# Routing of a mixture of experts: a moved square root, a comparison in another element order, added products and an early Gelu

## The chip, the cores and the metric

The kernel runs on one core of one Trainium2 chip. The metric is the device time of one execution in microseconds; lower is better. The engines of a core are TensorE (PE for its products, PEld for its weight loads), VectorE (DVE), ScalarE (ACT), GpSimd (POOL) and SyncE (SP, which here only issues DMAs). Each runs its own queue in order; semaphores tie them together.

## The reference

The input is x[2, 256, 64, 64]. Two layers follow: area attention with a gated recurrence, and convolutions with a state-space scan, then the mixture of experts that this change is about. Cut to that last part:

```python
# t: 8192 tokens of 256 values, E = 8 experts, hidden size 512
xf = (t - mean(t)) / sqrt(var(t) + 1e-5)           # per token
probs = softmax(xf @ gate_w + gate_b)              # [8192, 8]
top2_vals, top2_idx = top_k(probs, 2)
for e in range(8):
    h = gelu(xf @ W1[e] + b1[e])                   # exact Gelu
    out += weight_of_e[:, None] * (h @ W2[e] + b2[e])
t = t + out
```

## The kernel before

The experts are computed only for the tokens that chose them. Every token has two picks; the picks are laid out in blocks of 256 rows (`RB`), all rows of a block for one expert, at most 71 blocks (`NBLK`, rounded up to `NB` = 72), of which 68 are computed here. The part has four stages, all within `experts`.

**Normalise and choose** (`normalise`, `choose`). The tokens lie as 64 tiles of 128 (`TILES`), in 16 groups of four (`K`). Per group, `turn` transposes on PE and ACT copies the result to `x_turned`; `measure` takes the sums of the variance on DVE; `gates` multiplies four groups at a time by the gate's weights; `turn_gates` transposes these products back and DVE copies them to `logits`. For each half of the tiles, `root_in` computes the variance on DVE and its square root on ACT (L1818), and `root_out` the reciprocal. `scale` then normalises each group, three tiles of four on ACT (L1835) and one on POOL (L1831), and SP writes it to a table of rows in memory (`rows`, L1838). The order of all this is written out by hand (the engine queues follow the program). `choose` picks the two experts of each token on DVE.

**Slots.** Two products (L1972, operands `both` with `every` and `behind`) count how many tokens chose each expert before each token; from that DVE computes the slot of every pick: a block number `hi` and a place in the block `lo`. POOL then fetches the weights of the first three blocks (`wt`).

**The table loop** (L2030 to L2049). It inverts the slots: for each block and place, which token sits there. Sixteen rounds, each for four tiles. In a round DVE compares `hi` with the numbers 0 to 71 (`high`, L2033), ACT scales the result by the partition's number (L2038) and eight times by the tile's number (L2041) into `named`, DVE compares `lo` with the numbers 0 to 255 eight times (`low`, L2043), and PE multiplies `low` by `named` into `table` (L2045), 16 products. `high` and `named` have two buffers, `low` eight. These tiles take over the memory of the normalised tokens `xt`, so the first comparison waits until the last copy of tokens is written out.

```python
high = p4.tile([P, K, 2, NB], BF16, name="high")
nc.vector.tensor_tensor(
    high, place[:, :NB].unsqueeze(1).unsqueeze(1).to_broadcast([P, K, 2, NB]),
    hi[:, t0 : t0 + K].unsqueeze(3).to_broadcast([P, K, 2, NB]), ALU.is_equal,
)
```

Behind it `exponents` computes the softmax's exponentials on ACT (L1928 to L1930), and DVE turns the table into the indices `xi` and `ri`.

**Blocks and combination** (`run_blocks`, `combine`). For each block POOL gathers its tokens (`xg`), PE transposes them (`px`, L2085), DVE copies (L2087), PE multiplies by the first weights (`ph`, L2097) in four parts, ACT applies Gelu to each part (L2099), and PE multiplies by the second weights (`py`, L2107). The products of a block are interleaved with those of the block before it; the first block has none before it. A part's first product waits for the Gelu of the part before. At the end `combine` weighs the two results of each token and adds them to the input.

Of the kernel before, what the change touches and what calls it, by code (L numbers as in the profile page):

```python
# [10 lines left out]
F32 = mybir.dt.float32  # L11
BF16 = mybir.dt.bfloat16
I32 = mybir.dt.int32
AF = mybir.ActivationFunctionType
ALU = mybir.AluOpType
# [3 lines left out]
P = 128  # L19
# [13 lines left out]
E, HID = 8, 512  # L33

TB, RB = 512, 256


_WIDTHS = [
# [1648 lines left out]
def experts(tc, sh, ap, out, half, left):  # L1687
# [12 lines left out]
    nc, tok = tc.nc, sh.tok  # L1700
    NH, T, K = HID // P, B * N, TB // P
    NBLK = 2 * T // RB + E - 1
    TILES, J = T // P, RB // P

    OFTEN = 2 * T // RB + E // 2
    NB = NBLK + NBLK % 2
    with ExitStack() as ctx:
        cp = ctx.enter_context(tc.tile_pool(name="e_const", bufs=1))
# [16 lines left out]
        def iota(name, shape, pattern, base=0, step=0):  # L1725
            t = cp.tile(shape, F32, name=name)
            nc.gpsimd.iota(t, pattern, base=base, channel_multiplier=step, allow_small_or_imprecise_dtypes=True)
            return t
# [3 lines left out]
        numbers = iota("numbers", [P, RB], [[1, RB]])  # L1732
        place = cp.tile([P, RB], BF16, name="place")
        nc.vector.tensor_copy(place, numbers)
        me = iota("me", [P, 1], [[0, 1]], step=1)
        me1 = iota("me1", [P, 1], [[0, 1]], base=1, step=1)
# [3 lines left out]
        every = cp.tile([P, P], BF16, name="every")  # L1740
# [14 lines left out]
        wi = cp.tile([P, NBLK], I32, name="wi")  # L1755
        used = cp.tile([1, 1], I32, name="used")

        ex = cp.tile([P, TILES, E], F32, name="ex")
        best, total = (cp.tile([P, TILES], F32, name=n) for n in ("best", "total"))
        work = cp.tile([P, 2, TILES], F32, name="work")  # L1760
        held = ctx.enter_context(ExitStack())
# [10 lines left out]
        def normalise(p2, logits, halves):  # L1772


            with ExitStack() as own:
# [15 lines left out]
                def group(g):  # L1791
                    return slice(g * K, g * K + K)

                def turn(g):
                    turned = ps.tile([P, 2, K, P], F32, name="turned")
                    for c in range(2):
                        for k in range(K):
                            nc.tensor.transpose(turned[:, c, k], tok[:, g * K + k, c * P : c * P + P], sh.ident)
                    nc.scalar.copy(x[:, :, group(g)], turned)

                def measure(g):
                    for t in range(g * K, g * K + K):
                        for c in (0, 1) if t in left else (1,):
                            nc.vector.bn_stats(half[:, t, c], tok[:, t, c * P : c * P + P])

                def root_in(i):


                    at = slice(i * TILES // 2, (i + 1) * TILES // 2)
                    records = half[:, at].rearrange("p t c (i k) -> p t (c i) k", k=3)  # L1810
                    means, m, a = records[:, :, :, 1], mean[:, at], away[:, at]
                    nc.vector.tensor_reduce(m, means, AX.X, ALU.add)
                    nc.vector.tensor_scalar(m, m, 0.25, None, ALU.mult)
                    nc.vector.tensor_tensor(a, means, m.unsqueeze(2).to_broadcast([P, TILES // 2, 4]), ALU.subtract)
                    nc.vector.tensor_tensor(a, a, a, ALU.mult)
                    nc.vector.scalar_tensor_tensor(a, a, 64.0, records[:, :, :, 2], ALU.mult, ALU.add)
                    nc.vector.tensor_reduce(var[:, at], a, AX.X, ALU.add)
                    nc.scalar.activation(inv[:, at], var[:, at], AF.Sqrt, scale=1.0 / C, bias=sh.eps5)  # L1818

                def root_out(i):  # L1820
# [19 lines left out]
                def gates(q):  # L1840

                    pe = pg.tile([P, TB], F32, name="by_expert", bufs=2)
                    for c in range(2):
                        for j in range(4):
                            nc.tensor.matmul(
                                pe[32 * j : 32 * j + 32], gate[:, c], x[:, c, group(4 * q + j)],
                                start=c == 0, stop=c == 1, tile_position=(0, 32 * j),
                            )
                    return q, pe

                def take_gates(q, pe):
                    mine = pn.tile([P, TB], F32, name="by_expert_s", bufs=1)
                    nc.vector.tensor_copy(mine, pe)
                    return q, mine

                def turn_gates(q, mine):
                    pt = pg.tile([P, K, P], F32, name="by_token")
                    for k in range(K):
                        nc.tensor.transpose(pt[:, k], mine[:, k * P : k * P + P], sh.ident)
                    nc.vector.tensor_copy(  # L1860
                        logits[:, 16 * q : 16 * q + 16].rearrange("p (j k) e -> p j k e", k=K),
                        pt.rearrange("p k (j e) -> p j k e", e=32)[:, :, :, :E],
                    )
# [5 lines left out]
                for g in range(TILES // K):  # L1869
                    turn(g)  # L1870
                    if g == 4:
                        for i in range(8):
                            measure(i)
                        centre_gate()
                    if g == 5:
                        ready = take_gates(*gates(0))
                        root_in(0)
                        for i in range(8, 10):
                            measure(i)
                    if g == 6:  # L1880
                        turn_gates(*ready)
                    if g == 7:
                        root_out(0)
                        for i in range(10, 13):
                            measure(i)
                    if g == 9:
                        ready = take_gates(*gates(1))
                        for i in range(13, 16):
                            measure(i)
                    if g == 10:  # L1890
                        turn_gates(*ready)
                        halves[0]()
                    if g == 13:
                        ready = take_gates(*gates(2))
                        root_in(1)
                last = gates(3)
                turn_gates(*ready)
                ready = take_gates(*last)
                root_out(1)
# [26 lines left out]
        def exponents(pr):  # L1926

            nc.scalar.activation(one, going[:, 0, 0:1], AF.Exp)  # L1928
            nc.scalar.activation(ex, pr, AF.Exp)
            nc.scalar.activation(best, best, AF.Exp)  # L1930

        def weigh():
            nc.vector.tensor_reduce(total, ex, AX.X, ALU.add)
# [17 lines left out]
        def route():  # L1951
            with ExitStack() as own:
# [9 lines left out]
                p4 = own.enter_context(tc.tile_pool(name="e_r4", bufs=2))  # L1962
# [6 lines left out]
                rest = ps.tile([P, E * TILES], F32, name="rest")  # L1969
                turned = both.rearrange("p t e -> p e t")  # L1970
# [8 lines left out]
                n = p1.tile([P, E], F32, name="n")  # L1979
# [13 lines left out]
                at = left.rearrange("p t e -> p (t e)").rearrange("p (e t) -> p e t", e=E)  # L1993
                nc.vector.tensor_tensor(at.rearrange("p e t -> p (e t)"), scanned, rest, ALU.add)
                nc.vector.tensor_tensor(at, at, off.unsqueeze(2).to_broadcast([P, E, TILES]), ALU.add)
                at = at.rearrange("p e t -> p t e")
# [6 lines left out]
                hi = p1.tile([P, TILES, 2], BF16, name="hi")  # L2003
# [25 lines left out]

                table = ps.tile([P, J, 512], F32, name="table")  # L2030
                for t0 in range(0, TILES, K):
                    high = p4.tile([P, K, 2, NB], BF16, name="high")
                    nc.vector.tensor_tensor(  # L2033
                        high, place[:, :NB].unsqueeze(1).unsqueeze(1).to_broadcast([P, K, 2, NB]),
                        hi[:, t0 : t0 + K].unsqueeze(3).to_broadcast([P, K, 2, NB]), ALU.is_equal,
                    )
                    named = p4.tile([P, K, 2, 2, NB], BF16, name="named")
                    nc.scalar.mul(named[:, :, :, 1], high, me1)  # L2038
                    for t in range(t0, t0 + K):
                        for i in range(2):  # L2040
                            nc.scalar.mul(named[:, t - t0, i, 0], high[:, t - t0, i], float(t + TILES * i))  # L2041
                            low = p4.tile([P, RB], BF16, name="low", bufs=8)
                            nc.vector.tensor_scalar(low, place, lo[:, t, i : i + 1], None, ALU.is_equal)  # L2043
                            for j in range(J):
                                nc.tensor.matmul(  # L2045
                                    table[:, j, : 2 * NB], low[:, j * P : j * P + P],
                                    named[:, t - t0, i].rearrange("p k n -> p (k n)"),
                                    start=t == 0 and i == 0, stop=t == TILES - 1 and i == 1,
                                )  # L2049
                exponents(pr)  # L2050
                tile_of, inner = (table[:, :, k * NB : k * NB + NBLK] for k in range(2))
                tokens = p1.tile([P, J, NBLK], F32, name="tokens")
# [298 lines left out]
```

## Time and profile before

| | |
|---|---|
| median of 3 runs | 2871.01 us (2867.4 to 2874.39) |
| the profiled execution | 2871.29 us, span 2869.4 us |
| mean granted TensorE clock | 0.958 |
| busy: PE, DVE, ACT, POOL | 91%, 68%, 54%, 44% of the span |
| normalise and choose, slots | 2158.0 to 2218.45 us |
| table loop | 2218.45 to 2255.2 us |
| indices, first gathers, first blocks | 2255.2 to 2281.9 us |
| remaining blocks | 2281.9 to 2790 us |
| combination | 2790 to 2869.4 us |

Times in the profile are microseconds from the span's start. A row of a group or of the timeline gives when it starts, how long it was busy, the engine and the line, and in brackets how long its engine sat idle before it and what ended that. The granted clock is the share of full speed that TensorE was given. PE's busy share says little by itself, since products are pipelined.

### The profile page before, as it was taken

Reading aid. Unit: us, or ns where it says so; the run is one execution under the profiler, and the core shown is the slowest. Engines: PE = TensorE matmul, PEld = TensorE weight load, DVE = VectorE, ACT = ScalarE, POOL = GpSimd, SP = SyncE. Lnnn points to the kernel's source line nnn. Section 1 sums busy time; section 2 is a strip of 40 time slices with the busy share of each in tenths; the row PEclk is TensorE's granted clock in tenths of the full one; section 3 lists DMA queues with packets and bytes.
Section 4 is the critical chain, followed back from the end, with each engine's and each line's share of the span. In section 5 each row is a group of like instructions: output and inputs, shape, how many; then the busy total and the mean of one; then the engine's idle time right before and its main releaser. Section 6 shows DMA issues by size and latency. Waiting matters only on the chain.

```text
span 2869.4 us, 45738 instructions
## 1 busy us (share of the span) xinstructions
PE 2621.8 (91%) x17062; PEld 1502.7 (52%) x17062; DVE 1939.3 (68%) x3768; ACT 1542.8 (54%) x2623; POOL 1250.7 (44%) x1164
## 2 busy tenths in 40 slices
PE   7899999999999999997899999868895799999984
PEld 2233333333333333322899999724443588888873
DVE  4788888888888888886666667698887512221116
ACT  2567676776777676763444555576636522222223
POOL 1445445453544545452230000187761166666651
PEclk9999999999999999999899999999997799999995
DMA  3576767767767667777230000045543266666648
GB/s 133 102 138 124 139 129 133 139 130 133 137 132 135 131 130 140 133 140 144 84 155 1 1 2 1 12 124 137 143 129 138 85 222 232 220 234 220 233 171 342
DMA packets 104826, 388.15 MB, mean 135 GB/s; under 512 B 19656, under 2 KB 20560, under 8 KB 94864
## 3 DMA queue, kind: packets, MB, share of 16 engines
q0 software_dynamic: 71488, 293.00, 43.3%
q1 hardware_dynamic: 31872, 87.86, 9.5%
q10 hardware_dynamic: 1232, 4.25, 0.4%
q8 instruction: 137, 2.24, 0.3%
q14 instruction: 97, 0.79, 0.1%
HBM read 173.30 MB, written 43.58 MB: 76 GB/s over the span
## 4 chain that ended last, share of the span: by engine, by line
PE 77%; DVE 10%; issue 4%; DMA 3%; ACT 3%; POOL 2%; SPq 0%; ACTq 0%; DVEq 0%; POOLq 0%
PE ps L301 10%; PE ph L2097 9%; PE av_o L415 8%; PE py L2107 8%; PE po L169 8%; PE z L824 7%; PE ps L402 7%; PE z L836 7%; PE ps L397 3%; DVE hs L1569 2%; PE yp L1579 2%; DMA sx<-ex 2%; PE po L181 1%; PE px L2085 1%; PE po L415 1%
## 5 line engine op out<-in xcount | busy, mean ns | idle before, releaser
L371 DVE SCALAR_TENSOR_TENSOR acc<-vh,w_pe,acc 128x1008 f32<-128x1008 f32 (+7 forms) x384 | 483.3, 1262 | 8.3
L619 POOL DMA_DIRECT2D sx<-ex x320 | 276.8, 951 | 458.5 <-ACT ex L409 162.6
L409 ACT ACTIVATE ex<-ps 128x1024 f32<-128x1024 f32 x384 | 373.9, 1026 | 138.0 <-issue 56.1
L317 DVE CUSTOM_DVE_ANT_0 more<-ps,more 128x512 f32<-128x512 f32 x480 | 303.0, 687 | 132.5 <-PE ps L301 124.6
L2099 ACT ACTIVATE act<-ph,wt 128x256 f32<-128x256 f32 x272 | 128.9, 474 | 388.4 <-PE ph L2097 385.2
L2087 DVE COPY xt<-px 128x512 f32<-128x512 f32 x68 | 47.0, 692 | 397.7 <-PE px L2085 397.7
L2097 PE MATMUL ph<-xt,wt 128*128 128x256 f32 x1088 | 293.0, 392 | 4.9 <-ACT act L2099 3.0
L402 PE MATMUL ps<-q,k 32*128 32x512 f32 x2048 | 286.4, 602 | 0.0
L2107 PE MATMUL py<-wt,act 128*128 128x256 f32 x1088 | 279.6, 380 | 0.0
L614 POOL TENSOR_TENSOR sx<-sx,ex 128x1024 f32<-128x1024 f32 x64 | 152.3, 2380 | 220.7 <-PE ps L301 172.7
L313 ACT ACTIVATE more<-ps 128x1024 f32<-128x1024 f32 x240 | 233.5, 1029 | 18.1 <-ACT sx L409 5.9
L2097 PEld LDWEIGHTS ph<-xt,wt 128*128 128x128 f32 x1088 | 191.5, 192 | 68.0 <-DVE xt L2087 23.9
L824 PE MATMUL z<-xs,u 128*128 128x128 f32 x1872 | 223.2, 276 | 0.0
L415 PE MATMUL av_o<-ex,vt 128*32 128x512 f32 x1536 | 212.3, 609 | 6.1 <-ACT ex L409 5.9
L824 PEld LDWEIGHTS z<-xs,u 128*128 128x128 f32 x1872 | 216.9, 193 | 0.2 <-issue 0.2
L2107 PEld LDWEIGHTS py<-wt,act 128*128 128x128 f32 x1088 | 202.2, 191 | 24.9
L848 ACT ACTIVATE t<-z,bias 128x128 f32<-128x128 f32 x468 | 136.3, 361 | 145.8 <-PE z L836 145.7
L2122 POOL DMA_INDIRECT results<-y,ri x136 | 138.0, 1015 | 140.7 <-DVE y L2115 118.9
L301 PE MATMUL ps<-k,q 32*128 32x512 f32 x1088 | 195.6, 639 | 2.1 <-DVE nm L307 1.3
L836 PE MATMUL z<-xs,v 128*128 128x128 f32 x1512 | 179.6, 275 | 0.0
L836 PEld LDWEIGHTS z<-xs,v 128*128 128x128 f32 x1512 | 174.1, 192 | 0.2 <-DVE xs L855 0.2
L1576 POOL TENSOR_TENSOR cs<-hs,cs 128x1024 f32<-128x1024 f32 x63 | 148.6, 2361 | 55.1 <-DVE hs L1569 32.6
(432 smaller groups left out, 4530.5 us busy)
## 6 DMA issues: line engine op xcount, KB each, us to landing
sx<-ex POOLq DMA_DIRECT2D x320, 512.0 KB
cs<-c_rows SPq DMA_DIRECT2D x128, 256.0 KB
y<-results SPq DMA_DIRECT2D x32, 512.0 KB
x<-xrows SPq DMA_DIRECT2D x8, 1024.0 KB
rows<-xt SPq DMA_DIRECT2D x16, 512.0 KB
out_x<-res POOLq DMA_DIRECT2D x15, 512.0 KB
xrows<-xn SPq DMA_DIRECT2D x24, 256.0 KB
x<-in_x SPq DMA_DIRECT2D x4, 1024.0 KB
```

The costliest lines, as they stand in the source:

```text
L301: made.append(nc.tensor.matmul(tiles[h // 2][:, h % 2], qs[G, i // HM][head(h), i % HM * P : (i % HM + 1) * P], keys[head(h)], start=True, ...
L313: nc.scalar.activation(held["more"][j], tiles[j], AF.Relu)
L317: nc.vector.tensor_tensor_reduce(more, tiles[h // 2][:, h % 2], more, -1.0, 3.0e38, ALU.add, ALU.min, accum_out=nms[G][:, 0, h, i : i + 1],)
L371: mark(nc.vector.scalar_tensor_tensor(part, vh[:, c, 2 + r0 + dy : 2 + r1 + dy, w0 + dx : w1 + dx], w_pe[:, c, k : k + 1], part, ALU.mult, ...
L402: nc.tensor.matmul(tiles[h // 2][:, h % 2], k[head(h), m % HM * P : (m % HM + 1) * P], qs[G, n][head(h)], start=False, stop=True, tile_pos ...
L409: nc.scalar.activation(exs[i], tiles[i], AF.Exp, scale=HD**-0.5)
L415: nc.tensor.matmul(to[head(h)], lhs, exs[h // 2][:, h % 2], start=first, stop=last, tile_position=(0, HD * h))
L619: nc.gpsimd.dma_start(total[i], exs[i], accum_op=ALU.add)
L824: nc.tensor.matmul(z[c][:, g, :m], u[:, k, c, g], xt[:, k], start=g == GATES[0] and k == 0, stop=False, skip_group_check=True,)
L836: nc.tensor.matmul(z[c][:, g, :m], v[:, k, c, g], h[:, k], start=False, stop=k == 1, skip_group_check=True,)
L2097: nc.tensor.matmul(ph[:, hc], wt[:, at : at + P], xt[:, c], start=c == 0, stop=c == 1)
L2107: nc.tensor.matmul(py[:, j], act[:, hc, j * P : j * P + P], wt[:, at : at + C], start=hc == 0, stop=hc == NH - 1,)
```

## The change

Four things, all before the blocks:

- The square root of each half leaves `root_in` and becomes a function of its own, `root`. For the first half it is called right behind `root_in(0)`, as before. For the second it is called behind the last `gates`, so that on ACT it stands behind the copies of the last two groups.
- The comparison `high` is laid out with the 72 numbers outermost and the eight picks innermost. Its first operand is no longer a broadcast but a stored array `counted`, written once by POOL; it shares the memory of `ex`, which is used later. `high` being in another order, ACT reads it with a step of eight elements at both of its lines.
- Behind the table loop PE makes 28 products of `every` and `turned` (a view of `both`) into `rest`, whose value is not used any more.
- Behind the exponentials ACT computes a Gelu of a constant into a cell of `total`, which is overwritten later. The load of Gelu's table stands before it.

```diff
+WARM_UP = 28
...
-        ex = cp.tile([P, TILES, E], F32, name="ex")
+        held_by_both = cp.tile([P, 2 * TILES * E], BF16, name="ex")
+        ex = held_by_both.bitcast(F32).rearrange("p (t e) -> p t e", e=E)
+        counted = held_by_both[:, : NB * K * 2].rearrange("p (n k i) -> p n k i", k=K, i=2)
+        nc.gpsimd.tensor_copy(counted, numbers[:, :NB].unsqueeze(2).unsqueeze(2).to_broadcast([P, NB, K, 2]))
...
                     nc.vector.tensor_reduce(var[:, at], a, AX.X, ALU.add)
+
+                def root(i):
+
+                    at = slice(i * TILES // 2, (i + 1) * TILES // 2)
                     nc.scalar.activation(inv[:, at], var[:, at], AF.Sqrt, scale=1.0 / C, bias=sh.eps5)
...
                         root_in(0)
+                        root(0)
...
                         root_in(1)
                 last = gates(3)
+                root(1)
                 turn_gates(*ready)
...
             nc.scalar.activation(best, best, AF.Exp)
+            nc.scalar.activation(total[:, 0:1], sh.eps5, AF.Gelu)
...
-                    high = p4.tile([P, K, 2, NB], BF16, name="high")
+                    high = p4.tile([P, NB, K, 2], BF16, name="high")
                     nc.vector.tensor_tensor(
-                        high, place[:, :NB].unsqueeze(1).unsqueeze(1).to_broadcast([P, K, 2, NB]),
-                        hi[:, t0 : t0 + K].unsqueeze(3).to_broadcast([P, K, 2, NB]), ALU.is_equal,
+                        high, counted,
+                        hi[:, t0 : t0 + K].unsqueeze(1).to_broadcast([P, NB, K, 2]), ALU.is_equal,
                     )
                     named = p4.tile([P, K, 2, 2, NB], BF16, name="named")
-                    nc.scalar.mul(named[:, :, :, 1], high, me1)
+                    nc.scalar.mul(named[:, :, :, 1], high.rearrange("p n k i -> p k i n"), me1)
...
-                            nc.scalar.mul(named[:, t - t0, i, 0], high[:, t - t0, i], float(t + TILES * i))
+                            nc.scalar.mul(named[:, t - t0, i, 0], high[:, :, t - t0, i], float(t + TILES * i))
...
+                for _ in range(WARM_UP):
+                    nc.tensor.matmul(rest, every, turned, start=True, stop=True)
                 exponents(pr)
```

## The prediction

> **What bounds the kernel now.** I read the page's 40 slices first: TensorE is 90% busy everywhere except between slices 29 and 32 and at the end, and all edits lie in the first of these stretches (2158 to 2282 us), the experts' routing. A table of windows over it:
>
> ```profile
> 2158.00:2218.45 60.45, 32.90 (x214) 20.17 (x214) 46.33 (x162) 39.74 (x66) 11.30 (x20) 0.76 0.36 139
> 2218.45:2255.20 36.75, 24.59 (x256) 22.83 (x256) 35.93 (x144) 32.18 (x145) 2.39 (x3) 0.84 0.26 98
> 2255.20:2281.90 26.70, 15.64 (x38) 10.42 (x38) 3.15 (x8) 5.52 (x10) 8.52 (x9) 0.55 0.25 84
> 2281.90:2790.00 508.10, 506.10 (x2412) 415.66 (x2411) 110.61 (x170) 126.48 (x267) 321.97 (x334) 1.00 0.62 218
> ```
>
> Columns: stretch, length, busy PE, PEld, DVE, ACT, POOL, granted clock, DMA share, GB/s. The first row is normalising and choosing, the second the table loop, where DVE never rests (35.93 of 36.75), the third the first blocks at a clock of 0.55, the fourth the blocks, PE without a gap. Whatever the first three gain or lose arrives whole at the end. The chain of waits says what joins them:
>
> ```profile
> 2215.41 2.63 DMA rows<-xt
> ...
> 2218.45 0.76 DVE high L2033
> ...
> 2259.30 2.73 DMA xg<-rows,xi
> ...
> 2265.97 1.28 ACT L2099
> ```
>
> The loop starts when the last token copy has been written (its tiles take over that memory), not when DVE's own chain ends (2217.50); the blocks start when the gathers land; the first Gelu waits for a table load.
>
> **The square root.** The timeline before the loop:
>
> ```profile
> 2189.62 0.32 ACT L1818 ACTIVATE inv<-var,eps 128x32 f32<-128x32 f32 x1 [8.40 <-DVE var L1817]
> 2189.85 1.90 ACT L1799 COPY x_turned<-turned 128x1024 f32<-128x1024 f32 x2
> ...
> 2191.65 23.70 ACT L1835 ACTIVATE xt<-x,less,inv 128x256 f32<-128x256 f32 x48
> ```
>
> ACT waits 8.40 us at the second root (the first is not moved past anything) and holds two copies behind it; PE's last gate products wait 5.99 us for those. Moved behind them, the root still starts at 2189.62, when DVE has the variance, but the token copies follow at 2190.0: 1.65 us earlier. DVE gains more: it met the third turned gates at 2196.36 and would meet them at 2189.6, so the indices come about 6.7 us earlier, at 2210.7. That lets POOL issue the three weight gathers (3.5 MB) at about 2212 in place of 2217.74, and their data moved 1.8 us after the issue: at 2213.8, some 0.75 MB of token rows are still to be written at the 415 GB/s that the windows show as the most. Shared evenly the rows finish 1.3 us late. Bounds: -1.7 (no collision) to +1.5 (rows get a third); I take -0.4 us.
>
> **The comparison.** One of 16 rounds:
>
> ```profile
> 2236.41 0.74 DVE L2033 TENSOR_TENSOR high<-place,hi 128x576 bf16<-128x576 bf16 x1
> 2237.08 1.64 DVE L2043 TENSOR_SCALAR low<-place,lo 128x256 bf16<-128x256 bf16 x8
> 2237.25 0.78 ACT L2038 ACTIVATE named<-high,me 128x576 bf16<-128x576 bf16 x1 [0.24 <-PE table L2045]
> 2237.93 1.31 ACT L2041 ACTIVATE named<-high 128x72 bf16<-128x72 bf16 x8
> 2238.22 1.35 PE L2045 MATMUL table<-named,low 128*128 128x144 bf16 x16 [0.62 <-ACT named L2041]
> ```
>
> The round is 2.24 us, DVE's: 0.67 from `high` to the first `low`, then eight at 0.196. ACT needs 0.68 and eight at 0.1525, 1.90 us. At two elements a tick `high` loses 288 elements of 1.01 ns (744 ns for 576 against 304 for 142 at L2055): 0.29 us, a round of 1.95 on DVE, -4.6 us over 16 rounds, if ACT keeps 1.90. It may not. `high` now lies with its 72 numbers outermost, so ACT reads all 1152 elements of a round at a step of 8 bf16, 16 bytes. ACT has no such read in the trace; others have. The operand `both` of L1972 is read at just that step:
>
> ```profile
> L1972 PE MATMUL count<-both,every x1: 1057/1057/1057, 2205.1 to 2205.1; 128*128 128x512 bf16 x1
> ...
> L1558 PE MATMUL bn<-s_b,spread x128: 377/381/634, 1881.3 to 2145.4; 96*128 96x512 bf16 x128
> ```
>
> Minimum, median, maximum in ns. At half clock (0.50 in its window) the product with steps takes 1057 ns; a contiguous one of 512 columns takes 634 at most, its value at half clock: +0.83 ns an element. DVE's read in steps of 64 words at L1999 takes 1041 ns where L1995, contiguous and as long, takes 730: +0.61. PE's stationary loads at L743, also 64 words, come 146 ns apart at full clock against 109 contiguous: +0.29. ACT's round is then 2.24, 2.61 or 2.86 us; below, 1.90. Two of three say ACT takes the bound, and I take 0.70 ns, between them: 2.71 us, +0.47 in 16 rounds, **+7.5 us** (ends -4.6 and +9.9). PE (1.35 to 2.1 us a round) and DVE (1.95) hide under it. POOL's new copy of 576 numbers, about 1.3 us by its 555 ns for 256 elements, falls into POOL's idle 14.45 us before 2172.86: nothing; without that cover it would be those 1.3 us. Its result shares memory with `ex`, so the exponentials also wait for the last comparison, which is over 2 us before them.
>
> The Trainium skill (SBUF — State Buffer, in the section on door 1, the port swizzle) speaks against this edit and for it at once. It says lines are 16 bytes and an access to a new line each time pays, yet calls a step of eight bf16 free. L1972 decides that for PE: not free. Read the second way, the loop would bring -4.6 us and the sum would be 2865.6.
>
> **The products and Gelu's table.** 28 products of 512 columns go behind the table in PE's queue; the first block's transposes queue behind them. Let T be the loop's end. Before, PE waited 5.69 us and the second gather landed at T+6.84, so that much is free. How long are 28? Contiguous they came 0.22 us apart at full clock (6.2 us). But these read `both` at the 16-byte step: 0.88 apart at half clock (24.6 us). At full clock, 0.22 and DVE's +0.61 ns on 512 is 0.53: 14.8 us, which I take; PE ends the loop at 0.94 clock, so it starts warm. What a warm start is worth: before, the second block's first products began at T+21.55, still cold, and the three groups behind them took 5.09 us against 2.6 warm, as if begun warm at T+24.0. Warm, from the products' end: transposes 0.65, copy 0.79, three times products, Gelu and handoffs 1.59 (cold: 2.64), the last with the next transposes and copy 2.25: 8.5 us. So 14.8 + 8.5 - 24.0 = **-0.7 us**, ends -9.0 (6.5 us until PE is free) and +9.1 (24.6 us). Break-even is 0.55 us a product. In this is the moved table load: it runs at 2257.1, under ACT's idle 8.9 us, and takes 1.28 us off the first Gelu; if ACT were not idle it would only move. The first gather waits for ACT's exponentials, not for the new Gelu behind them.
>
> The Trainium skill (ScalarE: Activation LUTs, What ACT_TABLE_LOAD costs) adds a drain of 1.38 us to each load. Here the first Gelu starts 1.30 us after its load, so no drain shows; with it the sum would be 1.4 us lower.
>
> **Sum.** The profiled execution took 2871.29 us (span 2869.4 and 1.9 around it), 0.3 above the median of the runs. -0.4 + 7.5 - 0.7 = +6.4: **2877.7 us**.
>
> **Rivals.**
> 1. ACT reads steps at its old rate. DVE bounds the loop at 1.95: -4.6 - 0.4, with the products at 0.53 -5.7 (2865.6), at 0.22 -14.0 (2857.3). For: ACT has its own port, and no ACT read is shown to pay. Against: three reads on two engines that do. It turns to faster from a price below 0.29 ns.
> 2. The products keep the cold price, because the line sets it and not the clock (DVE's stepped read, 1.7 ns an element, is the same as PE's at half clock): +7.5 - 0.4 + 9.1 = +16.2, 2887.5. Against: L743 at full clock, 1.14 ns a column.
> 3. ACT pays L743's +0.29: round 2.24, loop unchanged, -1.1: 2870.2. The same comes if the comparison stays at one element a tick and ACT reads freely, so that the edit does not do what it says.
>
> **How the numbers follow.** Forecast 0.42 (its own range 2874 to 2883), rival 1 0.32, rival 2 0.15, rival 3 0.11. About 0.2% (5.7 us) can be told from no change. Slower: 0.39 of the forecast and rival 2, 0.54. Same: rival 3 and the forecast's low edge, 0.14. Faster: 0.32. The range reaches into both outer cases: 2859 to 2890.
>
> **What would show it.** ACT's root 0.3 us behind the two copies, `xt` from about 2190 after the same front; DVE idle before `high` by 5 us; weight gathers near 2212. `high` near 0.45 us; `named` at L2038's successor from 0.78 to some 1.2 us, its small ones from 246 to some 296, ACT without idle in the loop, DVE waiting. If `named` stays at 0.78, the third step is wrong and the loop is 32 us, not 44. The products' spacing tells rival 2: 0.53 or 0.88 or 0.22, and PE's idle before the first transpose should be gone. Blocks 0 and 1 at a clock near 1.0; below 0.7, the products bought nothing.

## The result and the profile after

The change makes the kernel slower: 2907.86 us (median of 4 runs, 2907.53 to 2908.34) against 2871.12 us for the kernel before in the same comparison (4 runs, 2867.4 to 2874.39). The ratio is 1.013, with a 95% interval of 1.0115 to 1.0144. The prediction said 2877.7, in a range from 2859 to 2890; it had the sign as its likeliest case and missed the size by 30 us. The profiled execution of the kernel after has a span of 2905.8 us.

The windows of the kernel after over the same part of the program (columns as before: stretch, length, busy PE, PEld, DVE, ACT, POOL, granted clock, DMA share, GB/s):

```profile
2218.00:2255.00 37.00, 22.56 (x176) 20.90 (x177) 27.01 (x106) 33.14 (x100) 0.00 (x0) 0.50 0.14 58
2255.00:2282.00 27.00, 22.52 (x97) 11.41 (x96) 11.72 (x45) 18.21 (x51) 0.00 (x0) 0.50 0.00 1
2282.00:2300.00 18.00, 13.80 (x16) 1.83 (x14) 0.00 (x0) 0.00 (x0) 2.98 (x4) 0.50 0.05 15
2300.00:2330.00 30.00, 26.52 (x93) 19.75 (x94) 2.93 (x5) 5.68 (x12) 10.19 (x11) 0.71 0.30 100
```

Two things are to be seen. The table loop, 36.8 us long before, runs into the second row, and in it the granted clock is 0.50 where it was 0.84. In the third row only PE works (13.80 of 18.00 us) and the clock stays at 0.50 under the very products that are added there; nothing is gathered until POOL's 2.98 us at its end.

The chain of waits names the places:

```profile
2211.27 9.69 DMA rows<-xt
2221.37 0.47 DVE high L2046
...
2268.09 2.08 PE table L2058 x16
2270.17 3.10 PE rest L2064 x4
2273.27 30.75 issue
2304.02 0.48 ACT act L2114
```

The last copy of token rows takes 9.69 us where it took 2.63. Behind the table stand the products `rest`, and the first Gelu (`act`) starts only at 2304.02. It now follows its product without a load of a table: that much of the change does what it says. The 30.75 us of "issue" is ACT's stretch before that Gelu, in which it waited for nothing that the profile shows; what was late must be read from the other engines. The timeline and the groups show it:

```profile
2187.30 0.32 ACT L1828 ACTIVATE inv<-var,eps 128x32 f32<-128x32 f32 x1 [4.59 <-DVE var L1823]
2187.52 1.57 ACT L1845 ACTIVATE xt<-x,less,inv 128x256 f32<-128x256 f32 x3
...
2221.37 0.46 DVE L2046 TENSOR_TENSOR high<-ex,hi 128x576 bf16<-128x576 bf16 x1 [12.24 <-DMA rows<-xt]
...
2296.11 0.95 POOL L1954 DMA_INDIRECT xg<-rows,xi  x1 [83.10 <-PE rest L2064]
...
2298.92 0.45 PE L2100 MATMUL px<-ident,xg 128*128 128x128 f32 x1 [3.57 <-DMA xg<-rows,xi]
```

```profile
L2054 ACT ACTIVATE named<-high 128x72 bf16<-128x72 bf16 x128 | 29.6, 312 | 0.0
L2064 PE MATMUL rest<-both,every 128*128 128x512 bf16 x28 | 25.4, 1078 | 0.0
L2051 ACT ACTIVATE named<-high,me 128x576 bf16<-128x576 bf16 x16 | 21.0, 1313 | 10.7 <-DVE high L2046 10.7
...
L2046 DVE TENSOR_TENSOR high<-ex,hi 128x576 bf16<-128x576 bf16 x16 | 7.2, 451 | 12.2 <-DMA rows<-xt 12.2
```

The same rows of the kernel before, and its first gather:

```profile
L2041 ACT ACTIVATE named<-high 128x72 bf16<-128x72 bf16 x128 | 21.0, 246 | 0.0
L2038 ACT ACTIVATE named<-high,me 128x576 bf16<-128x576 bf16 x16 | 12.4, 775 | 7.7 <-DVE high L2033 4.9 <-PE table L2045 2.7
L2033 DVE TENSOR_TENSOR high<-place,hi 128x576 bf16<-128x576 bf16 x16 | 11.9, 744 | 1.0 <-DMA rows<-xt 1.0
```

```profile
2258.05 0.95 POOL L1941 DMA_INDIRECT xg<-rows,xi  x1 [36.60 <-ACT best L1930]
```

The root is now followed at once by the token copies, as intended. A row that begins with a line number ends with busy time, mean ns of one, and the idle time of the engine before the group. The comparison `high` fell from 744 to 451 ns as foreseen, but ACT's two reads of it rose from 775 to 1313 and from 246 to 312 ns, and ACT has no idle time left but for the loop's start. And POOL's first gather, which before waited for ACT's exponentials, now waits for the last of the products.

**A scale for the parts.** The start of the second square root is released by DVE's variance in every kernel here. It lay anywhere from 2184.7 to 2193.3 us in the fourteen profiles, although no edit touches what stands before it except for a copy of 0.66 us on an idle POOL; that scatter is in every total. From that root on the stages repeat to about 0.1 us (0.7 in the loop where its last round ran at half clock), so the parts are compared there. The stages, in us, are differences of start times in each trace: root to the first `high`; to the end of the last `table` product; to block 0's first `ph`; to block 1's first `ph`; to the end. For the kernel after: 2221.37 − 2187.30 = 34.07, and so on.

| kernel | root to high | table loop | to block 0's ph | to block 1's ph | to the end | sum |
|---|---|---|---|---|---|---|
| before | 28.83 | 36.78 | 8.60 | 12.96 | 592.61 | 679.78 |
| after | 34.07 | 48.81 | 31.68 | 11.68 | 592.28 | 718.52 |
| e1_root | 33.74 | 36.73 | 8.55 | 12.95 | 590.26 | 682.23 |
| e2_compare | 28.84 | 48.84 | 8.56 | 12.96 | 589.86 | 689.06 |
| e3_products | 28.84 | 36.73 | 31.79 | 12.96 | 590.23 | 700.55 |
| e4_gelu | 28.83 | 36.79 | 8.59 | 11.68 | 590.37 | 676.26 |
| e5_flat | 28.83 | 37.52 | 13.22 | 12.96 | 592.73 | 685.26 |
| e6_step_elsewhere | 28.83 | 37.50 | 27.22 | 12.96 | 592.96 | 699.47 |
| e7_flat_elsewhere | 28.83 | 36.78 | 8.27 | 11.07 | 591.52 | 676.47 |
| e8_root_delayed | 27.02 | 36.87 | 8.57 | 12.95 | 589.90 | 675.31 |
| e9_pairs | 28.83 | 31.93 | 8.59 | 12.96 | 591.81 | 674.12 |
| e10_flat_gelu | 28.83 | 36.72 | 8.32 | 7.48 | 590.20 | 671.55 |
| e11_no_products | 27.02 | 32.05 | 8.57 | 11.68 | 592.52 | 671.84 |
| e12_all_mended | 27.03 | 32.05 | 8.21 | 7.48 | 589.71 | 664.48 |

The change adds 38.74 us behind the root: 5.24 before the loop, 12.03 in it, 23.08 between the table and block 0, −1.28 in block 0 and −0.33 behind. The last column moves by up to 3.3 us with the moment at which the clock comes up. In the kernel before that is between 2280 and 2284 us, where the granted clock is 0.83. Elsewhere, with the same products in the same order, it comes from 0.7 us ahead of block 1's first `ph` (e4) to 5.7 us behind it (e5), and half of such a delay is lost; in e10 and e12 the clock stays up through both blocks.

### The profile page after: what moved, and what is told of

Its sections match the earlier page's. It is cut to its first block, busy times and chain, and to the rows that moved or that the text cites. A ratio compares the mean times of both kernels' runs of the same rounds, so it can differ in the third digit from the quotient of the medians.

```text
span 2905.8 us, 45794 instructions
## 1 busy us (share of the span) xinstructions
PE 2651.5 (91%) x17090; PEld 1509.6 (52%) x17090; DVE 1940.3 (67%) x3768; ACT 1558.8 (54%) x2624; POOL 1252.8 (43%) x1165
## 3 DMA queue, kind: packets, MB, share of 16 engines
q8 instruction: 137, 2.24, 0.3%
## 4 chain that ended last, share of the span: by engine, by line
PE 77%; DVE 9%; ACT 4%; issue 4%; DMA 3%; POOL 2%; SPq 0%; DVEq 0%; POOLq 0%; ACTq 0%
PE ps L304 10%; PE ph L2112 9%; PE av_o L418 8%; PE py L2122 8%; PE po L172 8%; PE ps L405 7%; PE z L827 7%; PE z L839 7%; PE ps L400 3%; PE yp L1582 2%; DVE hs L1572 2%; DMA sx<-ex 1%; PE po L184 1%; PE po L418 1%; DVE more L320 1%
## 5 line engine op out<-in xcount | busy, mean ns | idle before, releaser
L1954 POOL DMA_INDIRECT xg<-rows,xi x136 | 130.2, 957 | 124.3 <-PE rest L2064 83.1
```

## The experiments

Each kernel was timed against the kernel before, whose medians in the three comparisons were 2870.0 (e1 to e4), 2867.6 (e5 to e7, e9) and 2868.06 us (e8, e10 to e12).

### One part of the change at a time

**e1_root**, the square root alone:

```diff
+                def root(i):
+                    at = slice(i * TILES // 2, (i + 1) * TILES // 2)
                     nc.scalar.activation(inv[:, at], var[:, at], AF.Sqrt, scale=1.0 / C, bias=sh.eps5)
...
+                        root(0)        # behind root_in(0)
...
+                root(1)                # behind the last gates
```

> Only the second square root moves. Theory (early weight gathers crowd out the last token rows): DVE's indices come some 6 to 7 us earlier, POOL issues the three weight gathers before the last two rows are written, the last row copy lands about 9 us after its issue in place of 2.6, and the first comparison starts about 5 us later than before: +5 us, 2876. Rival (the late landing in the changed kernel came from something else, such as the added POOL copy or the new memory of the comparison): the last rows land after 2.6 us and the loop starts 1.65 us earlier: -1.7 us, 2869.5.

Measured: 2873.36 us, ratio 1.001 (0.9998 to 1.0021). On ACT the edit does its work: `xt` starts 0.23 us behind the root, not 2.03 us. The chain and the DMA queues between 2213.5 us and the landing of the last row (packets, MB, share of the 16 engines; q0 are the gathers, q1 the rows):

```profile
2212.66 9.37 DMA rows<-xt
```

```profile
q0 software_dynamic: 298, 2.49, 82.2%
q1 hardware_dynamic: 152, 0.52, 15.0%
```

The three weight gathers are issued from 2210.8 us on, before the last rows are out, and the rows move 0.52 of 3.02 MB, 17% of the bytes. The engines are not shared evenly. `high` comes 4.91 us later than before, though the copies of tokens began 1.80 us earlier.

**e2_compare**, the comparison alone (`counted`, `high` with the numbers outermost, and the two reads of it, as in the change's diff):

> Only the comparison's order changes. Theory (ACT pays 0.93 ns for every element that it reads at a step of 16 bytes): the large scaling takes about 1.31 us in place of 0.775, the small ones 312 ns in place of 246, a round 2.97 us in place of 2.24, +11.8 us, 2883. Rival (the round is long because PE runs at half clock, and its products hold the buffers): ACT has idle time in every round, and the scalings that are long are those that wait; the round shortens where the clock is full.

Measured: 2882.29 us, ratio 1.0041 (1.0025 to 1.0056). Groups of the loop:

```profile
L2044 ACT ACTIVATE named<-high 128x72 bf16<-128x72 bf16 x128 | 29.9, 326 | 0.0
L2041 ACT ACTIVATE named<-high,me 128x576 bf16<-128x576 bf16 x16 | 21.2, 1324 | 3.6 <-DVE high L2036 3.6
L2036 DVE TENSOR_TENSOR high<-ex,hi 128x576 bf16<-128x576 bf16 x16 | 7.2, 452 | 1.0 <-DMA rows<-xt 1.0
```

The long read pays (1324 − 775) / 576 = 0.95 ns an element. The loop grows by 12.06 us, as much as in the whole change (12.03): ACT is its bound, and `high` meets the rows with only 1.0 us of waiting, so the two costs are separate.

**e3_products**, the 28 products alone:

```diff
+                for _ in range(28):
+                    nc.tensor.matmul(rest, every, turned, start=True, stop=True)
                 exponents(pr)
```

> Only the 28 products are added. Theory (the first gathers wait for the last product, since the memory of its operand belongs to the routing's pool, whose release they wait for; the stepped operand costs 0.9 us a product at any clock): 25 us of products, the gathers issued behind them, the first Gelu some 23 us later: +22 to +23 us, 2894. Rival (the price of a step falls with the clock): the loop ends at full clock here, products come 0.43 to 0.53 us apart, 12 to 15 us in all: +10 to +13 us, 2883.

Measured: 2889.94 us, ratio 1.0074 (1.0055 to 1.0093). Here the loop is the old one and ends at full clock. The windows around the products, and the products' line, of all 28 and of those that start before 2255 us (minimum, median and maximum ns, first and last start):

```profile
2248.00:2253.00 5.00, 3.45 (x34) 2.58 (x34) 4.04 (x18) 4.74 (x19) 0.00 (x0) 1.00 0.02 5
2252.00:2253.00 1.00, 1.00 (x6) 0.22 (x4) 0.65 (x3) 1.00 (x1) 0.00 (x0) 1.00 0.06 16
2254.00:2255.00 1.00, 1.00 (x3) 0.12 (x1) 0.22 (x1) 0.09 (x1) 0.00 (x0) 1.00 0.00 0
2256.00:2257.00 1.00, 1.00 (x2) 0.13 (x1) 0.00 (x0) 0.00 (x0) 0.00 (x0) 0.50 0.00 0
2258.00:2264.00 6.00, 6.00 (x8) 0.89 (x7) 0.00 (x0) 0.00 (x0) 0.00 (x0) 0.50 0.00 0
```

```profile
L2051 PE MATMUL rest<-both,every x28: 1058/1079/1079, 2252.1 to 2276.4; 128*128 128x512 bf16 x28
L2051 PE MATMUL rest<-both,every x4: 1058/1078/1079, 2252.1 to 2254.8; 128*128 128x512 bf16 x4
```

The first four products start at a clock of 1.00 and are already 0.90 us apart ((2254.8 − 2252.1) / 3), as are the later ones at 0.50 ((2276.4 − 2252.1) / 27 = 0.90). The clock does not set their price. Nor do they hold the clock: with PE busy without a gap it falls from 1.00 to 0.50 some 4 us behind their start.

**e4_gelu**, the constant's Gelu alone:

```diff
             nc.scalar.activation(best, best, AF.Exp)
+            nc.scalar.activation(total[:, 0:1], sh.eps5, AF.Gelu)
```

> Only the Gelu of a constant is added. Theory (the load moves under ACT's idle time): the first Gelu of the blocks starts right behind its product, -1.3 us, 2869.7. Rival (the gathers wait for ACT's last work, and so for the load): the first gather is issued 1.4 us later, 0 us.

Measured: 2867.41 us, ratio 0.9989 (0.9979 to 0.9999). In the table of stages only block 0 changes, by 12.96 − 11.68 = 1.28 us, the length of one table load; the other 2.24 us of this profile stand in the last column, where the clock comes up earlier. The four parts put together (4.91 + 12.06 + 23.19 − 1.28 = 38.88 us, each from the stage that it changes) give what the whole change shows in the same stages (39.07, the last column left out): next to nothing is due to the parts meeting. The medians alone would not show that: they add up to 33.0 us where the whole change has 36.7, with intervals of some 3 to 5 us either way on each part.

### The products: the step, the wait, and the clock

**e5_flat** reads the same memory in order; **e6_step_elsewhere** keeps the step but reads a constant tile that lives on; **e7_flat_elsewhere** does both. Each has the products alone:

```diff
-                    nc.tensor.matmul(rest, every, turned, start=True, stop=True)
+                    nc.tensor.matmul(rest, every, X, start=True, stop=True)
# e5: X = both.rearrange("p t e -> p (t e)")
# flat = going.bitcast(BF16).rearrange("p e t -> p (e t)")[:, : E * TILES]
# e6: X = flat.rearrange("p (t e) -> p e t", e=E)
# e7: X = flat
```

> The kernel before with the 28 products alone, their operand `both` read in order in place of steps of 16 bytes; the products' result is used by nothing. It lies in the same memory, so the first gather still waits for the last product. If the step alone makes a product cost 0.90 us whatever the clock, these come about 0.22 us apart at full clock, some 6.3 us in all, and the clock stays near 1.0 through them; the gathers then start about 4 us later than before, TensorE waits some 5 us for them and may grow cold again: between 2867 and 2875 us, that is at least 15 us less than the run with steps (2889.94). If the cost lies in products behind the table of any kind (0.90 us again, clock 0.50), it stays at 2890.

> The kernel before with the 28 products alone, still at steps of 16 bytes, but reading a constant tile (`going`) that lives on, so that the gathers' memory no longer waits for them; their result is used by nothing. If the late gathers are a term of their own, the products still take 25.2 us, the first gather goes at about 3 us behind the table as before, and the first transposes come right behind the last product: some 7 us less than with `both` in steps (2889.94), about 2883 us, and 13 above before. If the products alone hold up the first block and the gathers' wait is hidden, 2890.

> The kernel before with the 28 products alone, contiguous and from the constant tile: neither the step nor the gathers' wait; their result is used by nothing. They should take about 6.3 us in TensorE's idle time and end as the gathers land. If warm products shorten blocks 0 and 1, as step (c) of the prediction had it for its lower end (-9.0 with 1.3 of it from the Gelu), about -7.7: 2862 us, with a granted clock over 0.8 in the first block's products. If the waits inside blocks 0 and 1 let the clock fall anyway, within 2 us of before: 2868 to 2871.

Measured: e5 2874.59 us, ratio 1.0031 (1.0017 to 1.0044); e6 2886.23, 1.0061 (1.0048 to 1.0074); e7 2866.99, 0.9997 (0.9985 to 1.0009). Timeline rows of e5, then of e6, then of e7:

```profile
2251.76 6.47 PE L2051 MATMUL rest<-both,every 128*128 128x512 bf16 x27 [0.22 <-issue]
...
2258.98 0.95 POOL L1941 DMA_INDIRECT xg<-rows,xi  x1 [41.95 <-PE rest L2051]
```

```profile
2252.22 25.39 PE L2051 MATMUL rest<-going,every 128*128 128x512 bf16 x28
...
2255.24 0.95 POOL L1941 DMA_INDIRECT xg<-rows,xi  x1 [37.31 <-issue]
...
2277.70 1.09 PE L2087 MATMUL px<-ident,xg 128*128 128x128 f32 x4
```

```profile
2258.18 5.99 PE L2051 MATMUL rest<-going,every 128*128 128x512 bf16 x27
2264.28 0.30 PE L2087 MATMUL px<-ident,xg 128*128 128x128 f32 x1
```

In e5 the products come 0.22 us apart, but the gather still waits for the last of them. In e6 the gather goes 3 us behind the table, and PE, 25 us long at 0.90 us a product, transposes as soon as it is free. In e7 both are gone and the transposes follow the products at once. The column from the table to block 0's `ph` makes a square: 8.27 with neither, 13.22 with the held memory alone, 27.22 with the step alone, 31.79 with both. So the step costs 18.6 to 19.0 us and the held memory 4.6 to 5.0, and they add. What e5 gives up over e7 is a clock as well: PE waits 3.60 us for the gather behind its products and starts block 0 cold. By the profiles the chance that the wait is hidden (2890 for e6) is out. The medians do not decide it: e6 is 3 us above the expected 2883, and lies 18.6 us above its kernel before where e3 lies 19.9 above its own, with intervals that overlap. In the profiled execution e6's clock comes up late (592.96 in the last column, 590.23 in e3), which takes back 2.7 of the 4.57 us that it gains on e3 before block 0.

In e7 warm products are at last what they were meant to be, and the time is no better than before. Its windows show why:

```profile
2263.90:2267.31 3.41, 2.03 (x10) 1.12 (x8) 0.69 (x1) 0.00 (x0) 2.50 (x4) 1.00 0.38 109
2267.31:2270.72 3.41, 1.35 (x5) 0.68 (x4) 0.00 (x0) 1.89 (x3) 2.73 (x3) 1.00 0.52 118
2272.00:2276.00 4.00, 3.44 (x9) 2.16 (x9) 0.00 (x0) 0.61 (x2) 0.00 (x0) 0.50 0.54 220
```

Block 0 starts at 1.00, but PE is busy for only 2.03 and then 1.35 of 3.41 us, and at 2270.7 the clock falls. The longest single wait, 1.89 us for the first Gelu with its table load, lies in the second row. That this wait lets the clock fall is what e10 tests.

**e10_flat_gelu** takes the wait away: it adds the earlier load of Gelu's table to e7 (both edits as above):

> The kernel before with the contiguous products from the constant tile and the earlier load of Gelu's table; the products' result is used by nothing. Products alone left the clock at 1.00 until about 12 us behind the table, where it fell to 0.50 in the second group of the first block, behind a wait of 1.89 us for the first Gelu and its table load. If that wait is what lets the clock fall, the two together keep blocks 0 and 1 at a clock above 0.9 and bring what step (c) of the prediction put at its lower end, -9: 2859 us, more than the two apart (-0.6 and -2.6). If the handoffs of 0.56 us behind every Gelu let it fall all the same, the two add up: about 2864.

Measured: 2864.34 us, ratio 0.9983 (0.9972 to 0.9993).

```profile
2252.00:2258.00 6.00, 5.95 (x27) 2.48 (x26) 1.71 (x6) 3.23 (x6) 2.67 (x3) 1.00 0.14 38
2258.00:2268.00 10.00, 6.11 (x25) 3.96 (x26) 1.38 (x2) 1.89 (x4) 5.83 (x7) 1.00 0.58 201
2268.00:2280.00 12.00, 12.00 (x58) 10.02 (x58) 1.38 (x2) 2.97 (x7) 2.98 (x3) 1.00 0.11 24
```

The clock stays at 1.00 through both blocks. Block 0 takes 7.48 us in place of 12.96, while the Gelu load alone brought 1.28 and the products alone 1.89: 3.17 apart, 5.48 together. That the two depend on each other is shown by the profile (−8.23 us from the root on, near the expected −9). The median, −3.7, lies by the additive case (2864): at this scatter the times alone would not have told the cases apart.

### The other two parts mended

**e8_root_delayed** keeps the root's place and writes the weights' index behind the first `high`:

```diff
-                nc.vector.tensor_copy(wi, eb)
-                for i in range(3):
-                    fetch_weights(i)
...
+                    if t0 == 0:        # behind the first high
+                        nc.vector.tensor_copy(wi, eb)
+                        for i in range(3):
+                            fetch_weights(i)
```

> The kernel before with the square root moved alone, and the three weight gathers held back: their index is written behind the first `high` on VectorE, which waits for the token rows, so no gather runs beside the rows' writes. If the gathers crowded the rows out (last row 9.37 us in the run with the root alone, 2.63 before), the row is back at some 2.6 us and `high` comes 1.65 us earlier than before, as the prediction's front of the token copies had it: about 1.7 us under before, 2866 us. If the rows are late for another reason (their copies bunched on one queue), the row stays above 8 us and the time at that of the root alone, +3.

Measured: 2864.61 us, ratio 0.9995 (0.9985 to 1.0006). The chain:

```profile
2211.55 2.63 DMA rows<-xt
...
2214.59 0.77 DVE high L2035
```

The last row takes 2.63 us again, and `high` comes 1.81 us earlier than before. So the crowding came from the gathers; bunched row copies, the rival, are out.

**e9_pairs** keeps the pairs innermost, which DVE needs, and puts the 72 numbers next to them, so that ACT's step is 4 bytes and not 16:

```diff
-                    high = p4.tile([P, NB, K, 2], BF16, name="high")
+                    high = p4.tile([P, K, NB, 2], BF16, name="high")
                     nc.vector.tensor_tensor(
-                        high, counted,
-                        hi[:, t0 : t0 + K].unsqueeze(1).to_broadcast([P, NB, K, 2]), ALU.is_equal,
+                        high, counted.unsqueeze(1).to_broadcast([P, K, NB, 2]),
+                        hi[:, t0 : t0 + K].unsqueeze(2).to_broadcast([P, K, NB, 2]), ALU.is_equal,
                     )
...
-                    nc.scalar.mul(named[:, :, :, 1], high.rearrange("p n k i -> p k i n"), me1)
+                    nc.scalar.mul(named[:, :, :, 1], high.rearrange("p k n i -> p k i n"), me1)
```

(shown against the change's lines; the read at the second line of ACT changes likewise, `counted` holds 72 pairs, and the rest is the kernel before).

> The kernel before with the comparison alone, in another layout: the pairs innermost as in the change, but the 72 numbers outside them and the tiles outside those, so that ScalarE reads `high` at a step of 2 bf16 (4 bytes) in place of 16. VectorE's comparison should stay at 0.45 us. If the price is of the 16-byte step, ScalarE is back at some 0.78 and 0.246 us, the round is VectorE's 1.95 us, and the time is about 4.6 us under before: 2865.5. If any step costs ScalarE 0.9 ns an element, the round stays at 2.98 and the time at that of the comparison alone, 2882.3.

Measured: 2865.35 us, ratio 0.9993 (0.9983 to 1.0003).

```profile
L2044 ACT ACTIVATE named<-high 128x72 bf16<-128x72 bf16 x128 | 21.0, 247 | 0.0
L2041 ACT ACTIVATE named<-high,me 128x576 bf16<-128x576 bf16 x16 | 12.4, 775 | 3.6 <-DVE high L2036 3.6
L2036 DVE TENSOR_TENSOR high<-ex,hi 128x576 bf16<-128x576 bf16 x16 | 7.1, 446 | 1.1 <-DMA rows<-xt 1.1
```

ACT is back at 775 and 247 ns (775 and 246 before), DVE keeps 446, and the loop is 4.85 us shorter. The price belongs to the size of the step, not to a step.

**e11_no_products** has the edits of e8, e9 and e4 together; **e12_all_mended** adds that of e7:

> The kernel before with three parts mended and no products: root with the weight gathers held back (-1.7), the comparison with the pairs innermost and read at a step of 4 bytes (-4.6 by its rounds), the earlier load of Gelu's table (-2.6). If they add up, 2859 us; blocks 0 and 1 stay at half clock. If the shorter loop only shows the next wait (token rows, gathers), less of it arrives: 2863.

> The three mended parts with the contiguous products from the constant tile as well; the products' result is used by nothing. If the products together with the Gelu load keep the clock up, -1.7, -4.6 and -9: about 2853 us, some 6 under the run without products. If the clock falls in the first block anyway, within 2 us of the run without products.

Measured: e11 2861.78 us, ratio 0.9986 (0.9976 to 0.9996); e12 2854.91, 0.9963 (0.9951 to 0.9976). Up to block 1 e11 is 7.85 us shorter than before, as its three parts are apart (1.81 + 4.85 + 1.28 = 7.94): they add up, and the median, between the two cases expected, does not tell. From the root on e12 is 15.30 us shorter than before: 1.80 before the loop, 4.73 in it, 0.39 and 5.48 up to block 1, and 2.90 behind. The products bring 4.2 us of this in block 0 (11.68 against 7.48), and 6.9 us by the two medians, where about 6 was expected. e12 beats both kernels; by its ratio it is 0.24% to 0.49% faster than the kernel before.

## Why the prediction was wrong

By its own steps, in the stages of the table:

| step | predicted | measured |
|---|---|---|
| the root | −0.4 | +5.24 (root to `high`) |
| the comparison | +7.5 | +12.03 (loop) |
| products and Gelu | −0.7 | +21.5 (23.08 − 1.28 − 0.33) |
| place of the root itself | 0 | −2.3 (2189.62 to 2187.30, in no edit) |

That is 6.4 against 36.4, and 2905.8 − 2869.4 is 36.4. The sign of the total came out right through the comparison alone; the other two steps were forecast as small gains and cost 5 and 21 us.

**Products.** This step holds 22 of the 30 us, and three of its readings failed. First, the price: 0.53 us was taken as 0.22 at full clock and DVE's step price on top; it is 0.90, or 28 × 0.37 = 10.4 us more. The rival that kept the cold price, "because the line sets it and not the clock", was right; e3 shows 0.88 us for the first product at a clock of 1.00. Second, "the first gather waits for ACT's exponentials" held in e4 but not here. The products' operand `both` lies in memory that the blocks' gathered tokens take over, so the gathers wait for PE's last read of it: 4.6 to 5.0 us. The same rule stands in the prediction's own text, for `high` and the normalised tokens; it was not applied to the reader that the change adds. The rival with the right price shared this step and the next, and so stopped at 2887.5. Third, "it starts warm": the products were taken to carry the clock into the blocks. The start was cold already: the 0.94 had been read at the end of the old loop, and with the longer rounds the clock was 0.50 (2255 to 2282 us). But e3, where the loop ends at 1.00, shows that a warm start is lost under these products too. Taken out of 22.2 us, 10.4 and some 4.7 leave about 7 us for the blocks' cold start, which fits e10's 7.48 against 11.68 for block 0, 2.1 us in the last column and the transposes ahead of them.

The prediction's own sign of this, a clock "below 0.7, the products bought nothing", came true: it was 0.50 in block 0 (2301.86 to 2313.54 us).

**The comparison.** The mechanism was right: DVE's row fell to 451 ns, ACT became the bound without idle time, and the round grew. The price of a stepped read on ACT was the mis-sized term: 0.70 ns an element, put between three rows; it is (1313 − 775) / 576 = 0.93, above the highest of them (0.83). The round is 2.97 us in place of 2.71, and 16 of them make 4.2 of the missing 4.5 us. The rivals in which ACT reads freely, or at +0.29, are out.

On what the Trainium skill says (SBUF — State Buffer, the section on door 1): an access to a new 16-byte line pays, and a step of eight bf16 is still free. Two reads at just that step, PE's and ACT's, were slower here, and a step of two bf16 was free for ACT (775 ns, as contiguous). The first half of the rule agrees with the runs; its figure for bf16 does not.

**The root.** ACT's side was right, to the tenth: `xt` 0.22 us behind the root, and the weight gathers issued 22.07 us behind the root and not 28.12, 6.05 us earlier where 5.7 had been worked out. The share of the DMA engines was wrong. It was set at one half, with a third as the worst case; the rows got 17% of the bytes (e1). By the prediction's own figures, 0.75 MB at half of 415 GB/s, an even share makes the rows 1.8 us late and not 1.3, which changes little. The kernel before kept the two apart by accident: its first weight gather went out at 2217.74 us, when the last row (2215.41 and 2.63) was all but written.

**Gelu.** The 1.28 us were right.

**POOL's copy.** It took 0.66 us, half of what was worked out, at 2156.5 us on an idle engine, and nothing waited for it.

## What to carry to other kernels

An added reader holds its operand's memory: before work is put into a gap, look who takes that memory over next, and whether the wait lands on the transfer that ends the gap. Filling work is worth little if it does not stream, or if the next stage has a long wait of its own; here it took contiguous products and the early table load, and neither alone did it (handoffs of 0.56 us did no harm, a wait of 1.89 us did). When a chain is pulled earlier, ask what was waiting behind it by luck; and when a layout serves one engine, work out the step that it gives to every other reader, in bytes.

## What the runs showed of the hardware

**Products read at a step of 16 bytes did not hold the clock.** The moments at which the clock changes can be worked out from its mean in short windows. In e6:

```profile
2250.00:2250.50 0.50, 0.14 (x2) 0.14 (x2) 0.50 (x4) 0.50 (x4) 0.00 (x0) 0.91 0.00 0
2253.50:2254.00 0.50, 0.50 (x1) 0.00 (x0) 0.47 (x2) 0.05 (x1) 0.00 (x0) 0.68 0.00 0
2257.00:2257.50 0.50, 0.50 (x1) 0.00 (x0) 0.00 (x0) 0.00 (x0) 0.45 (x1) 0.73 0.59 213
```

It falls to 0.50 at 2250.41, rises to 1.00 at 2253.82 and falls at 2257.23: steps of 3.41 us. The stretch before the rise begins with the loop's last products; the one before the second fall holds nothing but stepped products, and so does the one before the fall in e3. The rest of the 25 us runs at 0.50. Six us of contiguous products, reading the same values, raised or kept the clock (e5, e7, e10). At 0.22 us for a contiguous product against 0.90, PE moves data in some 24% of the time at full clock (an estimate from these two). The Trainium skill (TensorE: Matmul & The Clock Gate, part 1) has the clock follow how busy the array has been in a window of about 3.4 us that runs freely. The runs show steps of that length, and agree with the rest only if "busy" means data moved and not an instruction in progress. How much of a window must be busy, no run here settles.

**One step size, two engines that pay.** At 16 bytes PE takes 0.90 us for 512 columns at granted clocks of 1.00 and 0.50 alike (1.76 ns each), and ACT 0.93 to 0.95 ns an element more than contiguous. ACT pays nothing at 4 bytes.

**Gathers of POOL's queue beat SP's row copies.** While both ran, 298 packets of the one passed for 152 of the other, and 2.49 MB for 0.52 (e1). The Trainium skill (DMA: Bandwidth & Descriptors, in the section on queues, rings and completion order) has each engine alternate between its queues by packets, not by bytes. The bytes agree in kind, since the gathers' packets are larger (8.4 KB against 3.4 KB). Two packets for one agree only if what the profile counts as a packet is not what the skill means by it, which no run here shows.
